# Six of the eight u blocks by a one-level Strassen product beside the first group's scores

## The chip, the cores and the metric

The kernel runs on one core of a Trainium2 chip. The metric is the device time of one launch in microseconds (us), as the median of several runs. All arithmetic is in float32.

## The reference, cut to what matters

Two layers over a graph of N = 4096 nodes with D = 512 features. The first is an attention layer whose scores get the adjacency matrix added twice, the second a two-step graph convolution; each has a residual and a layer norm.

```python
def _L0_gnn_ref(x, spatial_encoding, edge_encoding, Wq, bq, Wk, bk, Wv, bv):
    q = x @ Wq.T + bq
    k = x @ Wk.T + bk
    v = x @ Wv.T + bv
    a = q @ k.T * scale + spatial_encoding + edge_encoding
    attn = jax.nn.softmax(a, axis=-1)
    return attn @ v
def _L1_gnn_ref(x, adj, W1, b1, W2, b2):
    h = jax.nn.relu(adj @ (x @ W1) + b1)
    out = adj @ (h @ W2) + b2
    return out
x = _layernorm(x + _L0_gnn_ref(x, adj, adj, ...), axis=-1)
x = _layernorm(x + _L1_gnn_ref(x, adj, ...), axis=-1)
```

## The kernel before

The two projections of the scores are folded into one matrix: with m made of Wq and Wk, the scores of a block are x times u, where u = m applied to x, scaled, plus a bias (`ub_t`). u has eight blocks (`u_products(b)`, b = 0 to 7), one for each group of 512 rows of the result. A block is made by 16 matmuls of 512 columns: four output quarters o, four contraction pieces c. ScalarE moves each quarter from PSUM to SBUF with its bias (L190), and four subtractions (`combine_u`, L204) make of its quadrants B11, B12, B21 and B22 the sums T1 to T4. Block 0 stays in SBUF. Blocks 1 to 7 go through the tile `uo` to memory (`u_d`, L196) and come back seven operands at a time when their group begins (`load_operand`, L214). `uo` comes from a pool with one buffer (L133).

The scores themselves are one-level Strassen products. For each group g and each block d of 512 rows of x there are seven products k in `ORDER` = 1, 2, 6, 7, 5, 4, 3, each with a left operand out of plain quadrants of x (A11, A12, A22) and their sums (S1 to S4), and a right operand of u (B11, B21, B22, T1 to T4). `qk` (L344) makes half a product with two matmuls of 256 columns; the products add up in two PSUM banks, X for k = 1, 6, 5, 3 and Y for 2, 7, 4, and VectorE adds the running state of the bank to the right quadrant of the scores after each product (`qk_read`, L360). X has one buffer, and so has Y. For group 0 the sums S1 to S4 of each block d are made by VectorE (`form_s`, L225) from the loaded piece of x transposed (`XTS`, two buffers) and stored; later groups load them (`load_s`).

The order of the work is written out by hand. The main loop (from L1086) counts units. A unit has seven steps, a step is one half of a score product; two units make a score block, 16 units a group. `at(unit, n, f)` hooks a function to a step, and `work[unit] = units, items` gives a list of TensorE pieces with their costs, to be spread over so many units from there on: after each step as many are issued as keep the pace. Each engine runs its own instructions in the order in which the loop wrote them, and waits on semaphores where it needs another's result; so do the DMA queues of SP and GpSimd (POOL).

In group 0 the pieces beside the scores are the u products: blocks 1 to 5 in units 0 to 10, blocks 6 and 7 in units 11 to 17 (L816, L817). Unit 18 has none. After the last scores of group 0 (unit 15) its maxima are finished, transposed and spread (`turn_max` at unit 16, `spread_max` at unit 17), and for each pair q of score rows VectorE subtracts the maximum (`shift`), ScalarE takes the exponential (`exps`), GpSimd adds up the rows (`sums`) and makes the sums of a further Strassen product (`px_t2`), at places that the list `PREP` sets. From unit 19 on the products of the exponentials with x (`px_items`, L476, tile "p") fill the gaps, 224 pieces in 14 units; the tiles of x for them are loaded by `load_x` three phases ahead, into two pools of together four buffers (`xnp` with three, `xnp2` with one). In group 0, GpSimd and VectorE also make the row sums of x that these products need (`sum_x`, `row_parts`). At unit 18 the pools of the u stage are closed (`form.close()`), and the pools of the later stages take over their memory.

Of the kernel before, what the change touches and what calls it, by code (L numbers as in the profile page):

```python
# [11 lines left out]
F32 = mybir.dt.float32  # L12
AF = mybir.ActivationFunctionType
ALU = mybir.AluOpType
# [4 lines left out]
P = 128  # L19
# [5 lines left out]
def tile_graph_attention_then_gcn(  # L25
# [51 lines left out]
    nc = tc.nc  # L77
# [4 lines left out]
    NG = N // W  # L82
    NP = NT // 2
    HW = W // 2
    NCK = N // CW
    PER = W // P
    HALF_SCALE = 0.5 / math.sqrt(D)
# [14 lines left out]
    t_sb = const.tile([P, NT, H], F32, name="t_sb")  # L102
    c_sb = const.tile([P, NT], F32, name="c_sb")
    c0_t = const.tile([P, 1], F32, name="c0_t")
    ub_t = const.tile([P, ND], F32, name="ub_t")

    u_d = [dram.tile([P, 7, 2, HW], F32, name=f"u_d{g}") for g in range(NG)]
# [13 lines left out]
    att = ctx.enter_context(ExitStack())  # L121
# [2 lines left out]
    bcp = att.enter_context(tc.tile_pool(name="bcp", bufs=1, side="right"))  # L124
    small = att.enter_context(tc.tile_pool(name="small", bufs=4, side="right"))

    xnp = att.enter_context(tc.tile_pool(name="xnp", bufs=3, side="right"))
    form = ExitStack()
    mp = form.enter_context(tc.tile_pool(name="mp", bufs=1, side="right"))
    m_t = mp.tile([P, ND, D], F32, name="m_t")  # L130
    g_t = mp.tile([P, D], F32, name="g_t")
    xtp = form.enter_context(tc.tile_pool(name="xtp", bufs=2, side="right"))
    uop = form.enter_context(tc.tile_pool(name="uop", bufs=1, side="right"))  # L133

    def bank(tag, name, bufs=1):
        return psum.tile([P, W], F32, tag=tag, name=name, bufs=bufs)
# [10 lines left out]
    B11, B21, B22, T1, T2, T3, T4 = range(7)  # L147
    B12 = T4
    OPERANDS = {1: (A11, B11), 2: (A12, B21), 3: (S4, B22), 4: (A22, T4), 5: (S1, T1),
                6: (S2, T2), 7: (S3, T3)}  # L150
    ORDER = (1, 2, 6, 7, 5, 4, 3)

    FAST_V = range(NG - 2)
    QUARTER = {1: (0, 0), 2: (0, 0), 6: (1, 0), 7: (1, 1), 5: (1, 1), 4: (1, 0), 3: (0, 1)}
    L = {}
    UT, UO, XTS, SA, S, XN, CB, MB, MACC, LACC, O, OT, RL, XR, T = ({} for _ in range(15))


    def load_xts(b):
        XTS[b] = xtp.tile([P, ND, W], F32, tag="xt", name=f"xt{b}")  # L160
        nc.sync.dma_start(XTS[b], xT[:, ts(b, W)].rearrange("(c p) i -> p c i", p=P))

    def u_products(b):

        ps = {}

        def one(o, c):
            def go():
                if c == 0:
                    ps[o] = bank("o", f"psu{b}_{o}", 4)  # L170
                nc.tensor.matmul(  # L171
                    ps[o], m_t[:, c, ts(o, P)], XTS[b][:, c, :], start=c == 0, stop=c == ND - 1
                )
                if c == ND - 1:
                    if o == 0:
                        if b:
                            UO[b] = uop.tile([P, 7, 2, HW], F32, tag="ut", name=f"uo{b}")
                        else:
                            for k in ORDER:
                                new_operand(0, k)  # L180
                    pair = (B11, B12) if o < 2 else (B21, B22)
                    if b:
                        to = UO[b][:, pair[0] : pair[1] + 1 : pair[1] - pair[0], o % 2, :]
                        todo = [(to, ps[o].rearrange("p (h i) -> p h i", h=2))]
                    else:
                        todo = [
                            (UT[0, pair[h]][:, o % 2, :], ps[o][:, ts(h, HW)]) for h in range(2)
                        ]
                    for to, src in todo:
                        nc.scalar.activation(  # L190
                            to, src, AF.Identity, bias=ub_t[:, o : o + 1], scale=HALF_SCALE
                        )
                    if o == ND - 1:
                        if b:
                            combine_u(nc.gpsimd, {k: UO[b][:, k] for k in range(7)})
                            nc.gpsimd.dma_start(u_d[b], UO[b])  # L196
                        else:
                            combine_u(nc.vector, {k: UT[0, k] for k in range(7)})

            return go  # L200

        return [one(o, c) for o in range(ND) for c in range(ND)]

    def combine_u(eng, ut):  # L204
        for out_, a, b_ in ((T1, B12, B11), (T2, B22, T1), (T3, B22, B12), (T4, B21, T2)):
            eng.tensor_tensor(ut[out_], ut[a], ut[b_], ALU.subtract)
# [204 lines left out]

    def load_x(n):
        g, a, b, k = PHASES[n]
        pool = xnp2 if n % 4 == 3 else xnp
        XN[n] = pool.tile([P, b - a, 2 * P], F32, tag="xn", name=f"xn{n}")
        plain = {1: (0, 0), 2: (1, 0), 4: (1, 1)}
        if k in plain:
            t, f = plain[k]
            src = x.rearrange("(d t j p) f -> t p d j f", p=P, t=2, j=2)[t]
            for d in range(a // 2, b // 2):  # L420
                nc.sync.dma_start(
                    XN[n][:, 2 * d - a : 2 * d - a + 2], src[:, d, :, ts(f, 2 * P)]
                )
        else:
            nc.sync.dma_start(XN[n], xs_d[a][:, {6: 0, 7: 1, 3: 2, 5: 3}[k]])
# [282 lines left out]
    with tc.tile_pool(name="wqk", bufs=1) as wp:  # L708
# [52 lines left out]
        for w_t, w_n in ((wq_t, wq_n), (wk_t, wk_n)):  # L761
            for o in range(ND):
                ps = bank("o", f"psw{o}", 4)
# [43 lines left out]
    def at(unit, n, f, *args):  # L807
        n += unit * len(ORDER)
        hooks[n // len(ORDER), n % len(ORDER)].append(lambda: f(*args))
# [3 lines left out]
            f()  # L813

    work = {}
    work[0] = 11, [(0.86, f) for g in range(1, 6) for f in u_products(g)]  # L816
    work[11] = 7, [(0.86, f) for g in range(6, NG) for f in u_products(g)]  # L817
    for g in range(2, NG):
        at(max((g - 1) * ND * ND // 7 - 1, 0), 0, load_xts, g)

# [144 lines left out]
    def strassen(n, beside, done=()):  # L965
# [54 lines left out]
        (6, MID), (7, MID), (8, EARLY), (8, LATE), (9, MID), (10, MID), (11, MID), (12, MID),  # L1020
    ]

    PREP_LAST = [
        (1, (2, 2, 3)), (1, (3, 4, 4)), (1, (5, 6, 6)), (2, EARLY), (2, LATE), (3, LATE), (4, MID),
        *PREP[7:],
# [8 lines left out]
    for g in range(NG):  # L1034
        s0 = g * NP
        s1 = s0 + NP
        if g:
            for n, k in enumerate(ORDER):
                at(s0 - 2 + (2 * n + 1) // 7, (2 * n + 1) % 7, load_operand, g, k)
            at(s0 - 2 - (g == 1), 1, add_c0, g)  # L1040
            at(s0 - 2 - (g == 1), 3, row_consts, g)
        for q in range(NP):
            d, j = divmod(q, 2)
            if (g or d) and j == 0:
                early = 2 + (g == 1 and d == 0)
                at(s0 + q - early, 4, begin_scores, g, d)
                at(s0 + q - early, 5, add_scores, g, d)
            for h in range(2):
                n = 1 + 3 * (2 * j + h) if d < NP // 2 - 1 else 2 * j + h
                at(s0 + 2 * d + 2 + n // 7, n % 7, new_max, g, q, h)  # L1050
            unit, (n0, n1, n2) = (PREP_LAST if g == NG - 1 else PREP)[q]
            at(s1 + unit, n0, shift, g, q, 0)
            at(s1 + unit, n1, shift, g, q, 1)
            at(s1 + unit, n1, exps, g, q)
            at(s1 + unit, n2, sums, g, q)
            at(s1 + unit, n2, px_t2, g, q)
        at(s1, 5, turn_max, g)
        at(s1 + 1, 1, spread_max, g)
        if g < NG - 1:
            at(s1 + 13, 4, row_sums, g)  # L1060
        at(s1 + 14, 0, load_rows, g)
        at(s1 + 15, 0, add_bv, g)
        px = px_items(g)
        if g == NG - 1:
            for n, (u, k) in enumerate(spare):
                px.insert((8, 14, 20, 26, 90, 150)[n], (0.86, lambda u=u, k=k: product(u, k)))
        if g:
            px.reverse()
            by = 3 if g == NG - 1 else 1
            items = row_items(g - 1, lambda n: [px.pop() for _ in range(n * by)])  # L1070
            work[s1 + 1] = NP, items + px[::-1]
        else:
            work[s1 + 3] = NP - 2, px

    for n in range(3):
        at(NP + 1, 2 + n, load_x, n)

    last_unit = (NG + 1) * NP + 1
    at(last_unit - 5, 0, lambda: [sum_t(0, 0, 8), sum_t(8, 8, 14)])
# [6 lines left out]
    for unit in range(last_unit):  # L1086
        if unit == NP + 2:
            form.close()
            wvp = att.enter_context(tc.tile_pool(name="wvp", bufs=1, side="right"))
            bv_t = wvp.tile([P, D], F32, name="bv_t")  # L1090
            b2_t = wvp.tile([P, D], F32, name="b2_t")
            wv_t = wvp.tile([P, ND, D], F32, name="wv_t")
            w1_t = wvp.tile([P, ND, H], F32, name="w1_t")
            wvs_t = wvp.tile([P, 3, 2, HW], F32, name="wvs_t")
            v = wv_t.rearrange("p (f c) (h o) -> p f h c o", f=2, h=2)
            WV = {B11: v[:, 0, 0], T3: v[:, 0, 1], B21: v[:, 1, 0], B22: v[:, 1, 1]}
            WV.update({b: wvs_t[:, n] for n, b in enumerate((T1, T2, T4))})
            rowp = att.enter_context(tc.tile_pool(name="rows", bufs=1, side="right"))
            xnp2 = att.enter_context(tc.tile_pool(name="xnp2", bufs=1, side="right"))
        if unit == NP + 6:  # L1100
            nc.sync.dma_start(wv_t, wvT.rearrange("(c p) o -> p c o", p=P))
            nc.sync.dma_start(w1_t, w1.rearrange("(c p) h -> p c h", p=P))
# [36 lines left out]
    g = NG - 1  # L1139
# [171 lines left out]
```

## Time and profile before

| | us |
|---|---|
| median of 3 runs | 2329.12 |
| lowest and highest | 2328.04, 2330.17 |
| the profiled execution, its time | 2332.29 |
| its span, first to last instruction | 2330.5 |
| TensorE busy | 2298.2 |
| mean granted TensorE clock | 0.998 |

The page gives busy times of five engines: PE is TensorE's matmuls, PEld its weight loads, which overlap them, DVE VectorE, ACT ScalarE, POOL GpSimd; SP only issues transfers. A line of a group of instructions reads: line of the code, engine, operation, tile written and tiles read, shapes, count, then busy time and the mean in ns of one, then the idle time of the engine just before them and what ended it. In an order in time each line begins with the start and the duration in us, neighbours of one kind merged, and ends with the idle time before it in brackets, with its releaser. Numbers of buffers are left out of the names: `X` and `Y` are the score banks, `psu` the banks of the u products, `uo` the u tile on its way to memory, `p` the banks of the px products, `s` the score tiles.

### The profile page before, as it was taken

What the parts mean: (1) busy time and instruction counts of PE and PEld (TensorE: products, weight loads), DVE (VectorE), ACT (ScalarE), POOL (GpSimd) and SP (SyncE); (2) the same over time, 40 slices, a digit from 0 to 9 for tenths busy, and PEclk for the clock granted to TensorE, in tenths of its full rate; (3) what the DMA queues carried; (4) which work ended last, traced back from release to release, by engine and by line L of the source; (5) the groups of instructions that cost most, each with busy time, mean ns of one, the idle gap of its engine ahead of it and who ended that gap; (6) DMA issues with size and microseconds to landing.
All of it is one profiled execution on the core that took longest, in us unless ns stands there. A gap on an engine that the chain in (4) does not pass through costs nothing.

```text
span 2330.5 us, 28148 instructions
## 1 busy us (share of the span) xinstructions
PE 2298.2 (99%) x10518; PEld 1725.5 (74%) x10518; DVE 1615.2 (69%) x2270; ACT 399.1 (17%) x417; POOL 1004.8 (43%) x999
## 2 busy tenths in 40 slices
PE   9999999999999999999999999999999999999998
PEld 5666788888888888888888888888886743333456
DVE  4556665677678766865776676667757877888874
ACT  2111211131122112211311131121102100000012
POOL 1567654165328423741662185237419830011043
PEclk9999999999999999999999999999999999999999
DMA  5889787757757784778577667757654558899996
GB/s 155 261 279 306 230 228 192 220 146 218 216 154 210 199 233 131 216 193 232 129 233 200 180 188 202 226 144 216 185 184 157 179 218 311 330 354 371 344 387 224
DMA packets 276886, 523.27 MB, mean 225 GB/s; under 512 B 19152, under 2 KB 126416, under 8 KB 275856
## 3 DMA queue, kind: packets, MB, share of 16 engines
q1 hardware_dynamic: 229040, 406.12, 51.8%
q0 software_dynamic: 42176, 105.39, 20.5%
q10 hardware_dynamic: 5536, 9.97, 1.2%
q8 instruction: 84, 1.38, 0.2%
q14 instruction: 50, 0.41, 0.1%
HBM read 473.44 MB, written 46.40 MB: 223 GB/s over the span
## 4 chain that ended last, share of the span: by engine, by line
PE 91%; DVE 4%; POOL 2%; issue 1%; DMA 1%; ACT 0%; POOLq 0%; SPq 0%; DVEq 0%; ACTq 0%
PE p L491 31%; PE X L351 18%; PE b L957 14%; PE Y L351 13%; PE psu L171 4%; PE v L618 3%; PE acce L1256 2%; PE ops L1210 1%; PE tps L664 1%; PE x L566 1%; DVE s L441 1%; PE x1ps L655 1%; DVE s L364 1%; PE psm L774 1%; DVE s L446 1%
## 5 line engine op out<-in xcount | busy, mean ns | idle before, releaser
L491 PE MATMUL p<-s,xn 128*128 128x256 f32 x3584 | 895.5, 380 | 8.9 <-DVE s L441 5.9
L491 PEld LDWEIGHTS p<-s,xn 128*128 128x128 f32 x3584 | 677.7, 190 | 113.3 <-DVE s L441 9.1
L351 PE MATMUL X<-ut,sa 128*128 128x256 f32 x1984 | 513.8, 382 | 3.2 <-DVE s L364 3.2
L351 PEld LDWEIGHTS X<-ut,sa 128*128 128x128 f32 x1984 | 371.0, 190 | 87.8 <-issue 25.1
L407 POOL TENSOR_TENSOR lacc<-lacc,s 128x512 f32<-128x512 f32 x240 | 345.6, 1440 | 199.8 <-ACT s L398 188.9
L364 DVE TENSOR_TENSOR s<-X,s 128x512 f32<-128x512 f32 x256 | 176.2, 688 | 292.4 <-PE X L351 288.4
L351 PE MATMUL Y<-ut,sa 128*128 128x256 f32 x1408 | 360.9, 379 | 2.2 <-DVE s L364 1.8
L351 PEld LDWEIGHTS Y<-ut,sa 128*128 128x128 f32 x1408 | 266.3, 190 | 49.2 <-issue 12.2
L398 ACT ACTIVATE s<-s 128x1024 f32<-128x1024 f32 x128 | 135.2, 1057 | 803.4 <-DVE s L394 803.4
L373 DVE TENSOR_TENSOR macc<-macc,s 128x512 f32<-128x512 f32 x240 | 254.2, 1059 | 1.2
L364 DVE TENSOR_TENSOR s<-Y,s 128x512 f32<-128x512 f32 x192 | 132.0, 688 | 174.9 <-PE Y L351 174.1
L295 POOL DMA_DIRECT2D s<-in_adjT_dram x64 | 84.5, 1320 | 362.9 <-ACT s L290 359.1
L394 DVE TENSOR_TENSOR s<-s,mb 128x512 f32<-128x512 f32 x256 | 232.1, 916 | 2.5 <-ACT mb L321 2.5
L464 DVE TENSOR_TENSOR ot<-p,ot 128x512 f32<-128x512 f32 x248 | 169.0, 681 | 30.4 <-PE p L491 30.0
L924 DVE TENSOR_TENSOR tt<-ck 128x1024 f32<-128x1024 f32 x112 | 138.5, 1270 | 40.6 <-PE b L957 36.5
L957 PE MATMUL b<-tt,st 128*64 128x512 f32 (+1 forms) x768 | 156.1, 541 | 0.0
L171 PE MATMUL psu<-xt,m_t 128*128 128x512 f32 x256 | 128.0, 592 | 0.0
L441 DVE TENSOR_TENSOR s<-s 128x512 f32<-128x512 f32 x128 | 126.4, 1010 | 0.0
L434 POOL TENSOR_TENSOR s<-s 128x256 f32<-128x256 f32 x128 | 123.0, 961 | 0.6
L290 ACT COPY s<-cb 128x2048 f32<-128x2048 f32 x64 | 120.9, 1888 | 0.5
L957 PEld LDWEIGHTS b<-tt,st 128*64 128x64 f32 x768 | 53.9, 137 | 87.8 <-issue 79.4
L435 POOL TENSOR_TENSOR s<-s 128x256 f32<-128x256 f32 x128 | 107.1, 837 | 10.0
(165 smaller groups left out, 1971.6 us busy)
## 6 DMA issues: line engine op xcount, KB each, us to landing
ck<-in_adjT_dram SPq DMA_DIRECT2D x128, 1024.0 KB, 7.4
s<-in_adjT_dram POOLq DMA_DIRECT2D x64, 1024.0 KB, 11.6
sa<-s_d SPq DMA_DIRECT2D x224, 256.0 KB, 5.4
xn<-in_x_dram SPq DMA_DIRECT2D x192, 256.0 KB, 3.8
xn<-xs_d SPq DMA_DIRECT2D x96, 512.0 KB, 4.7
sa<-in_xT_dram SPq DMA_DIRECT2D x168, 256.0 KB, 4.7
xn<-xs_d SPq DMA_DIRECT2D x64, 256.0 KB, 4.0
u_d<-uo POOLq DMA_DIRECT2D x7, 1792.0 KB, 7.3
```

Of the source, the lines that this page charges most:

```text
L171: nc.tensor.matmul(ps[o], m_t[:, c, ts(o, P)], XTS[b][:, c, :], start=c == 0, stop=c == ND - 1)
L351: nc.tensor.matmul(T["X" if k in (1, 6, 5, 3) else "Y"][:, ts(j, HW)], SA[g, d, a][:, c, j, :], UT[g, b][:, c, :], start=k in (1, 2, 7) an ...
L364: nc.vector.tensor_tensor(ck, ps, ck, ALU.add)
L373: nc.vector.tensor_tensor(MACC[g], MACC[g], ck[:, h, :], ALU.max)
L394: nc.vector.tensor_tensor(ck, ck, MB[g], ALU.subtract)
L398: nc.scalar.activation(ck, ck, AF.Exp, scale=2.0)
L407: nc.gpsimd.tensor_tensor(LACC[g], LACC[g], ck[:, h, :], ALU.add)
L441: nc.vector.tensor_tensor(b, b, t2, ALU.subtract)
L464: nc.vector.tensor_tensor(to, ps, to, ALU.add)
L491: nc.tensor.matmul(T["PX" if k in (1, 6, 5, 3) else "PY"][:, ts(f, HW)], XN[n][:, q - a, ts(f, P)], quarters(g, q)[{1: 0, 2: 2, 6: 1, 7: 0 ...
L924: nc.vector.tensor_tensor(t[:, :2], v[:, :, 1], v[:, 0], ALU.subtract)
L957: nc.tensor.matmul(BK[n][k][ts(half, HH)], lhs, right(u, i, half, b), start=q == 0, stop=q == NP - 1,)
```

## The change

Blocks 2 to 7 of u are no longer made by `u_products` but by `u_fast`: seven products of quadrants of x with quadrants of m, with the same left sums S1 to S4 that the scores of group 0 use for the same block of x, and with sums of m as right operands. Each half of a product is two matmuls of 256 columns. Two banks add up as in `qk`, and after each product its state is read into or added to a quadrant: by ScalarE where it is the first to write there (k = 1, 6, 7, 3), by VectorE where it adds (k = 2, 5, 4). The last read of a block is put off to the first piece of the next (`owing`). GpSimd makes T1 to T3 as before, VectorE T4. The u tile is split: B11 has a tile of its own with two buffers, the other six operands share one with one buffer, and `store_u` sends both.

`m_sums` makes T1, T2 and T4 of m on GpSimd at unit 1, `m_t3` makes T3 in place on VectorE at unit 3. Block 1 is made as before, in units 0 to 2; blocks 2 to 7 in units 3 to 15. The px products of group 0 begin a unit sooner and take 15 units, the first two pairs of `PREP` are moved to unit 17 for group 0, block 1 of group 1's scores is begun a unit sooner, and of the four buffers for tiles of x two are now in each pool.

```diff
-    xnp = att.enter_context(tc.tile_pool(name="xnp", bufs=3, side="right"))
+    xnp = att.enter_context(tc.tile_pool(name="xnp", bufs=2, side="right"))
...
+    ms_t = mp.tile([P, 2, 2, HW], F32, name="ms_t")
...
+    def new_uo(b, what):
+
+        if what == B11:
+            UO[b] = {B11: uop.tile([P, 2, HW], F32, tag="b11", name=f"b11_{b}", bufs=2)}
+        else:
+            UO[b]["all"] = uop.tile([P, 6, 2, HW], F32, tag="ut", name=f"uo{b}")
+            UO[b].update({k: UO[b]["all"][:, k - 1] for k in range(1, 7)})
+
+    def store_u(b):
+        nc.gpsimd.dma_start(u_d[b][:, B11], UO[b][B11])
+        nc.gpsimd.dma_start(u_d[b][:, 1:], UO[b]["all"])
+
+    def m_sums():
+
+        m = m_t.rearrange("p (f c) (h o) -> p f h c o", f=2, h=2)
+        for k, v in ((B11, m[:, 0, 0]), (T3, m[:, 0, 1]), (B21, m[:, 1, 0]), (B22, m[:, 1, 1])):
+            MV[k] = v
+        MV[T1] = t_sb[:, 28:32, :].rearrange("p (c a) b -> p c (a b)", c=2)
+        MV[T2], MV[T4] = (ms_t[:, n] for n in range(2))
+        for out_, a, b_ in ((T1, T3, B11), (T2, B22, T1), (T4, B21, T2)):
+            nc.gpsimd.tensor_tensor(MV[out_], MV[a], MV[b_], ALU.subtract)
+
+    def m_t3():
+
+        nc.vector.tensor_tensor(MV[T3], MV[B22], MV[T3], ALU.subtract)
+
+    def u_fast(b):
+
+
+        X = {}
+
+        def read(k):
+            ps = X["X" if k in (1, 6, 5, 3) else "Y"].rearrange("p (o i) -> p o i", o=2)
+            if k == 1:
+                new_uo(b, B11)
+            if k == 6:
+                new_uo(b, "all")
+            to = UO[b][{1: B11, 2: B11, 6: B12, 4: B12, 7: B22, 5: B22, 3: B21}[k]]
+            if k in (1, 6, 7, 3):
+                for n in range(2):
+                    o = n + 2 * (k in (7, 3))
+                    nc.scalar.activation(
+                        to[:, n, :], ps[:, n], AF.Identity, bias=ub_t[:, o : o + 1], scale=HALF_SCALE
+                    )
+            else:
+                nc.vector.scalar_tensor_tensor(to, ps, HALF_SCALE, to, ALU.mult, ALU.add)
+            u = UO[b]
+            if k == 4:
+                for out_, a, b_ in ((T1, B12, B11), (T2, B22, T1), (T3, B22, B12)):
+                    nc.gpsimd.tensor_tensor(u[out_], u[a], u[b_], ALU.subtract)
+            if k == 3:
+                nc.vector.tensor_tensor(u[T4], u[B21], u[T2], ALU.subtract)
+                store_u(b)
+
+        def one(k, j):
+            def go():
+                if j == 0 and k in (1, 2, 7):
+                    X["X" if k == 1 else "Y"] = bank("o", f"psu{b}_{k}", 4)
+                for c in range(2):
+                    nc.tensor.matmul(
+                        X["X" if k in (1, 6, 5, 3) else "Y"][:, ts(j, HW)],
+                        MV[OPERANDS[k][1]][:, c, ts(j, P)],
+                        SA[0, b, OPERANDS[k][0]][:, c],
+                        start=k in (1, 2, 7) and j == 0 and c == 0,
+                        stop=c == 1,
+                        skip_group_check=True,
+                    )
+                if j == 0:
+                    if k == 1:
+                        if owing:
+                            owing.pop()()
+                    else:
+                        read(ORDER[ORDER.index(k) - 1])
+                elif k == 3:
+                    owing.append(lambda: read(3))
+
+            return go
+
+        return [one(k, j) for k in ORDER for j in range(2)]
...
-        pool = xnp2 if n % 4 == 3 else xnp
+        pool = xnp2 if n % 4 > 1 else xnp
...
-    work[0] = 11, [(0.86, f) for g in range(1, 6) for f in u_products(g)]
-    work[11] = 7, [(0.86, f) for g in range(6, NG) for f in u_products(g)]
+    work[0] = 3, [(0.86, f) for f in u_products(1)]
+    work[3] = 13, [(0.86, f) for g in range(2, NG) for f in u_fast(g)] + [(0, lambda: owing.pop()())]
+    at(1, 0, m_sums)
+    at(3, 0, m_t3)
...
+    PREP_FIRST = [(1, (2, 3, 4)), (1, (4, 5, 6)), *PREP[2:]]
...
-                early = 2 + (g == 1 and d == 0)
+                early = 2 + (g == 1 and d < 2)
...
-            unit, (n0, n1, n2) = (PREP_LAST if g == NG - 1 else PREP)[q]
+            unit, (n0, n1, n2) = {0: PREP_FIRST, NG - 1: PREP_LAST}.get(g, PREP)[q]
...
-            work[s1 + 3] = NP - 2, px
+            work[s1 + 2] = NP - 1, px
...
-        at(NP + 1, 2 + n, load_x, n)
+        at(NP + n // 2 + 1, 2 + n if n < 2 else 0, load_x, n)
...
-            xnp2 = att.enter_context(tc.tile_pool(name="xnp2", bufs=1, side="right"))
+            xnp2 = att.enter_context(tc.tile_pool(name="xnp2", bufs=2, side="right"))
```

More of the change, by code (lines that the diff above doesn't have):

```diff
@@ L155, in tile_graph_attention_then_gcn @@
     L = {}
+    MV, owing = {}, []
     UT, UO, XTS, SA, S, XN, CB, MB, MACC, LACC, O, OT, RL, XR, T = ({} for _ in range(15))
@@ L176, in go @@
                         if b:
-                            UO[b] = uop.tile([P, 7, 2, HW], F32, tag="ut", name=f"uo{b}")
+                            new_uo(b, B11)
+                            new_uo(b, "all")
                         else:
@@ L181, in go @@
                     pair = (B11, B12) if o < 2 else (B21, B22)
[L182 to L189, printed above, removed]
-                        nc.scalar.activation(
-                            to, src, AF.Identity, bias=ub_t[:, o : o + 1], scale=HALF_SCALE
+                    for h in range(2):
+                        nc.scalar.activation(
+                            (UO[b][pair[h]] if b else UT[0, pair[h]])[:, o % 2, :],
+                            ps[o][:, ts(h, HW)],
+                            AF.Identity,
+                            bias=ub_t[:, o : o + 1],
+                            scale=HALF_SCALE,
                         )
@@ L194, in go @@
                         if b:
-                            combine_u(nc.gpsimd, {k: UO[b][:, k] for k in range(7)})
-                            nc.gpsimd.dma_start(u_d[b], UO[b])
+                            combine_u(nc.gpsimd, UO[b])
+                            store_u(b)
                         else:
```

## The prediction

> **What bounds the kernel now.** First the page, for the engine that sets the end.
>
> ```profile
> PE 2298.2 (99%) x10518; PEld 1725.5 (74%) x10518; DVE 1615.2 (69%) x2270; ACT 399.1 (17%) x417; POOL 1004.8 (43%) x999
> ...
> PE 91%; DVE 4%; POOL 2%; issue 1%; DMA 1%; ACT 0%; POOLq 0%; SPq 0%; DVEq 0%; ACTq 0%
> ...
> L171 PE MATMUL psu<-xt,m_t 128*128 128x512 f32 x256 | 128.0, 592 | 0.0
> ```
>
> TensorE is idle for 32 us of 2330.5 and carries 91% of the chain that ended last: taking products away shortens the run unless waits fill the place. Matmul durations on the page are latencies of a pipelined unit; what one costs is the spacing of starts, so next the order in time on TensorE (start us, us, ... xcount, idle before):
>
> ```profile
> 32.45 10.46 PE L171 MATMUL psu<-xt,m_t 128*128 128x512 f32 x24
> 42.75 1.03 PE L351 MATMUL X<-ut,xt 128*128 128x256 f32 x4
> ```
>
> 24 records in 10.30 us are 0.429 us each. A float32 matmul makes two records (L171 counts 256 for the 8 x 16 matmuls of the code), so one of 512 columns costs 0.858 us. Now the same view where the u products end and the attention-times-x products ("p") begin:
>
> ```profile
> 251.91 1.03 PE L351 MATMUL X<-ut,sa 128*128 128x256 f32 x4
> 253.72 1.99 PE L351 MATMUL X<-ut,sa 128*128 128x256 f32 x8 [0.78 <-DVE s L364]
> 255.55 1.89 PE L351 MATMUL Y<-ut,sa 128*128 128x256 f32 x8
> 257.28 1.89 PE L351 MATMUL X<-ut,sa 128*128 128x256 f32 x8
> 260.96 1.99 PE L351 MATMUL Y<-ut,sa 128*128 128x256 f32 x8 [1.79 <-DVE s L364]
> 262.79 1.03 PE L491 MATMUL p<-s,xn 128*128 128x256 f32 x4
> ```
>
> From 255.55 to 257.28 eight records take 1.73 us: a matmul of 256 columns costs 0.4325 us. And unit 18 (from 253.72), the one unit with nothing beside the scores, shows what such a unit suffers: VectorE can't read the score banks in time, 0.78 and 1.79 us. The busy time by stretch, columns as in the page (us, then PE, PEld, DVE, ACT, POOL busy, clock, DMA share, GB/s):
>
> ```profile
> 150.00:200.00 50.00, 49.29 (x176) 33.05 (x176) 32.30 (x53) 7.93 (x9) 31.47 (x31) 1.00 0.87 267
> ...
> 254.00:276.00 22.00, 18.88 (x86) 15.95 (x86) 19.22 (x19) 6.02 (x6) 21.05 (x18) 1.00 0.75 223
> ```
>
> While u is made, TensorE is full and VectorE 65% busy; around unit 18 VectorE is 87% busy and TensorE loses 3 us of 22. Last, the tile that u passes through on its way to memory:
>
> ```profile
>   DMA u_d<-uo: 50.0, 4
> ...
> DMA to landing us min/median/max: 6.5/7.3/10.1
> ```
>
> ScalarE waited 50 us in four pieces for the store of the previous block to free the one buffer. No stall of TensorE goes with them: between 42 and 232 us it shows one, 0.71 us.
>
> **What the Trainium skill says.** "TensorE: Matmul & The Clock Gate", section "What's actually happening": after an idle window of about 3.4 us the array's clock is halved until it has been busy for as long. The trace has such a piece: after a 1.92 us wait at 301.34 ten records take 3.46 us (302.26 to 305.72) instead of 10 x 0.216 = 2.16, so a drop cost 1.3 us; the idle time before it was shorter than a window. "SBUF — State Buffer", section "Who interferes with whom": a VectorE instruction with two SBUF inputs and a GpSimd instruction that reads SBUF shut each other out. The trace agrees: the running maxima (L373) take 0.68 us alone and 1.06 on average.
>
> **The change, part by part.**
>
> (a) TensorE work. Per block, 16 matmuls of 512 columns (16 x 0.858 = 13.73 us) become 7 products x 2 halves x 2 = 28 of 256 (28 x 0.4325 = 12.11). The saving is 1.62 us, for six blocks 9.7 us. All of it lies where TensorE is full, so it counts whole: -9.7.
>
> (b) Reads of the u banks. ScalarE: 8 activations of 256 columns (0.47 us each, the row of ut) = 3.8 us a block in place of 4 x 0.69 = 2.7; it is below 20% busy here, nothing. VectorE gains three reads of PSUM plus SBUF (0.69, as L364) and one subtraction of two SBUF tiles (1.06, as L373): 3.1 us per block of 14 x 1.80 = 25.2 us, so its share goes from 65% to 77%. GpSimd loses one of four subtractions (1.6) and gains three once (4.8 us, in the second unit). Their cover is TensorE's other items: a product is read while the scores and the next product run, and its bank is written again at the earliest two items, 3.6 us, later. The tight place is the border of two score blocks, where the one X bank is read by VectorE with one u item (0.87 us) between. The trace of before has one stall there in 16 units, 0.71 us. With 12 points more load I take one more, 0.7 us (bounds 0 and 4); the wait of VectorE for the last plain u matmul before it overwrites m: 0.4.
>
> (c) The wait of ScalarE for the store. The six derived tiles still have one buffer. From the end of block b's last product: GpSimd is through with T1 to T3 after 2.7 us, the B11 store's issue 0.6, the large store's landing 7.3, ScalarE's next read 0.9: 11.5 us. TensorE needs that read at the fifth product of block b+1, eight items on: 8 x 1.80 + 0.87 = 15.3 us. Slack 3.8. For block 6, four subtractions of the row sums stand before the store on GpSimd (3.5 us): slack 0.3, I take a stall of 0.3. From block 1, still made the old way: after ScalarE 0.9, three subtractions 4.6, issues 1.2, landing 7.3, read 0.9 and a few tenths of signals, 15.3, against 17 pieces x 0.866 = 14.7: 0.6. Behind the waiting read on ScalarE stand the copies that begin later scores, needed two units on. So (b) and (c): +2.0, bounds 0 and 6.
>
> (d) Units 16 to 18. Before, 32 u items fill units 11 to 17, unit 18 is bare. Now u ends with unit 15, units 16 and 17 are bare (0.866 us a step), and the p products start with unit 18. Walk VectorE's order from the end of the last u product (T = 0), TensorE otherwise continuous: last X read till -0.1; a maximum till 1.0; T4, which waits for GpSimd's subtractions (second done at 1.1, third at 2.7), till 1.9 or 3.5; a maximum till 2.8 or 4.4; first read of the new X till 3.5 or 5.1, wanted at 3.56; two maxima till 5.0 or 6.7; the transposes of the maximum, wanted at 4.5 or 6.0, wait 0.5 to 1.3. Together 1.3 (T4 waits for two) or 3.0 (for three). In unit 17 the subtraction of the row maximum needs its broadcast through TensorE and ScalarE; four of them (0.68 each, 0.97 on average in this stretch) and four reads then fill VectorE, so the last X read comes 0.9 to 2.0 late. Sum 2.2 to 5.0, I take 3.6. In its place go 0.39 (a load, in unit 16) + 0.78 + 1.79 = 2.96. Net +0.6, bounds -0.8 and +2.
>
> (e) What moves without a price. The loads of x tiles keep four buffers in all (3 + 1 becomes 2 + 2); the third is loaded at unit 18 from a pool that waits for block 7's store, about 14 us after T = 0 and before unit 18 ends up needing it; behind it on SP stand loads wanted a unit later. The score loads of block 1 of group 1 start a unit sooner. The p products of group 0 are spread over 15 units instead of 14, the same number; the waits at 273.78, 277.47 and 301.34 (1.33, 0.83, 1.92) come from the hand-over from GpSimd to VectorE in two-row phases and stay. SP's loads of score operands for units 16 and 17 have less time per product (1.73 us against 7.0 to 7.5 to land), but stand seven products ahead, 12 us.
>
> Sum: -9.7 + 2.0 + 0.6 = -7.1 us. The span 2330.5 becomes 2323.4; with the 1.8 us outside the span (2332.3) the profiled run is 2325.2; the median lies 3.2 below its profiled run, so 2322.0.
>
> **The rivals.** *The bare units cost more.* For: three waits there pass from engine to engine, and idle pieces in sequence can bring the clock down. Against: unit 18 of before had 2.6 us of stalls at full clock. Price: 5.0 + two drops of 1.3 in place of 2.96, i.e. +4.6, and +2: -3.1, time 2326.0.
>
> *The store decides (slower).* If the one buffer comes free too late, TensorE stops in each of the six hand-overs. It needs the large store to land 7.3 + 3.8 = 11.1 us after its issue before TensorE loses anything; to end over 0.2% slower (+4.7) it has to lose 14.4 us, 2.4 per hand-over, a landing of 13.5 us, or 12.2 if each stall also brings a clock drop. For it: DMA is 87% busy here, and the 1 MB accumulating loads take 11.6. Against: seven stores took 6.5 to 10.1. Time at 13.5: 2334.
>
> *Everything fits.* No stall while u is made, unit 16 to 18 at the lower bound, and 1.5 us of the waits after 270 gone because the p products start more slowly: -9.7 - 0.8 - 1.5 = -12, 2317.1.
>
> **How the numbers follow.** Forecast 0.58, bare units 0.22, store 0.10, all fits 0.10. A measurement of this kernel tells 0.2%, 4.7 us, from no change. Forecast and "all fits" are faster: 0.68; bare units fall within: 0.22; the store is slower: 0.10. The range takes in the first, second and nearly the last: 2317.0 to 2330.0, the upper end being all upper bounds of (b) to (d) with some clock drops (-9.7 + 6 + 2 + 2.6 = +0.9).
>
> **What would show it.** The matmul group of u: 6 x 56 = 336 records of 256 columns, 64 of 512. Unit 18 starts some 7 us before 253.72. No wait of TensorE on ScalarE's or VectorE's u reads over 1 us; stalls of 2 to 5 us between the last u product and the first p product, named after VectorE. The time from the first p product to the end equal to before's within 2 us. I am wrong if TensorE waits in most hand-overs of u blocks, if the clock in that stretch falls below 0.97, or if the stretch after 330 us changes.

## The result, and the profile after

| | before | changed |
|---|---|---|
| median, us | 2329.70 (22 runs) | 2326.43 (22 runs) |
| lowest and highest | 2327.59, 2333.14 | 2323.25, 2328.72 |
| profiled execution: time, span | 2332.29, 2330.5 | 2326.35, 2324.6 |

The ratio of the changed kernel to the one before is 0.9984, with a 95% interval of 0.9977 to 0.999: 3.3 us less between the medians, where 7.1 were forecast. It lies in the range, but under the 0.2% that the forecast's own case called for. The first pair of profiles shows 5.9 us; the kernel before had been profiled in an execution 2.6 us above its median.

The page of the changed kernel, busy times and the chain:

```profile
PE 2288.3 (98%) x10662; PEld 1752.4 (75%) x10662; DVE 1631.5 (70%) x2295; ACT 403.7 (17%) x445; POOL 1006.0 (43%) x1003
...
PE 90%; DVE 4%; POOL 3%; issue 1%; DMA 1%; ACT 0%; POOLq 0%; SPq 0%; DVEq 0%; ACTq 0%
```

TensorE's busy time fell by 9.9 us, about what the products should give (9.7), the span by 5.9. So 4 us came back as idle time. Below is TensorE's order in time in the changed kernel: its longer waits from the u stage (the stretch in which u is made) up to the start of the p products.

```profile
183.90 1.28 PE L431 MATMUL X<-ut,xt 128*128 128x256 f32 x4 [2.09 <-DVE s L444]
184.97 1.91 PE L224 MATMUL psu<-xt,m_t 128*128 128x256 f32 x4
186.68 1.76 PE L431 MATMUL X<-ut,xt 128*128 128x256 f32 x4
188.28 1.03 PE L224 MATMUL psu<-xt,m_t 128*128 128x256 f32 x4
...
211.04 1.13 PE L431 MATMUL X<-ut,xt 128*128 128x256 f32 x4 [1.03 <-DVE s L444]
...
227.13 1.13 PE L224 MATMUL psu<-sa,t_sb 128*128 128x256 f32 x4 [2.87 <-ACT uo L206]
...
242.77 1.13 PE L431 MATMUL X<-ut,sa 128*128 128x256 f32 x4 [1.37 <-DVE s L444]
244.51 0.66 PE L458 MATMUL mt<-ident,macc 128*128 128x128 f32 x4 [0.60 <-DVE macc L453]
...
254.58 1.13 PE L431 MATMUL X<-ut,sa 128*128 128x256 f32 x4 [0.78 <-DVE s L444]
255.54 1.03 PE L571 MATMUL p<-s,xn 128*128 128x256 f32 x4
```

Unit 18 begins at 254.58, not 7 us before the 253.72 of the kernel before, but 0.9 us after it: all of the saving was gone by then. Yet p begins with it, in a unit that had been bare, and from there the changed kernel gains.

Two kinds of hand-over took the saving: from 40 to 239 us TensorE waits 4.1 us for VectorE to read the X bank, and 3.4 us for ScalarE to read a u bank. After the first long wait the clock dropped as well: the twelve records from 183.90 to 188.28 take 4.38 us, where twelve take 12 x 0.2165 = 2.60 elsewhere in this stretch (four in 0.866). That is another 1.8 us.

The ScalarE waits come from the tile of u on its way to memory:

```profile
  DMA u_d<-uo: 36.1, 4
...
DMA to landing us min/median/max: 5.8/10.2/10.9
```

The stores land after 10.2 us in the median (7.3 before). GpSimd's order between blocks 6 and 7 shows the hand-over with the longest wait, and the fence after it ScalarE's read that waited:

```profile
206.90 2.95 POOL L214 TENSOR_TENSOR uo<-uo 128x512 f32<-128x512 f32 x2
209.78 1.32 POOL L375 DMA_DIRECT2D s<-in_adjT_dram  x1
210.63 1.23 POOL L354 TENSOR_TENSOR t_sb<-t_sb 128x256 f32<-128x256 f32 x1
...
215.47 0.55 POOL L175 DMA_DIRECT2D u_d<-uo  x1
```

```profile
226.24 1.57 ACT L206 ACTIVATE uo<-psu,ub_t 128x256 f32<-128x256 f32 x4 [12.32 <-DMA u_d<-uo]
```

The subtractions for T1 to T3 end at 209.85, but the large store is issued only at 215.47, behind the issue of a 1 MB load and four subtractions of the row sums. It lands 10.7 us later, ScalarE goes on at 226.24, and TensorE stops for 2.87 us. The landing is not what sets this hand-over apart: the large stores of blocks 3 to 5 landed after 10.6, 10.9 and 10.2 us, with waits of at most 0.55 us on TensorE. But block 5's, for one, was issued 1.0 us after its last subtraction (181.30 to 182.32), block 6's 5.6 us after. Why the landings grew from 7.3 us is not shown.

The other place is the border of two score blocks, where the X bank passes from one to the next. VectorE's order at the one of 183.90:

```profile
178.43 1.74 DVE L453 TENSOR_TENSOR macc<-macc,s 128x512 f32<-128x512 f32 x1
180.09 0.68 DVE L444 TENSOR_TENSOR s<-Y,s 128x512 f32<-128x512 f32 x1
181.33 0.69 DVE L216 TENSOR_TENSOR uo<-uo 128x512 f32<-128x512 f32 x1 [0.56 <-POOL uo L214]
181.94 0.68 DVE L410 SCALAR_TENSOR_TENSOR t_sb<-t_sb,g_t 128x512 f32<-128x512 f32 x1
...
182.55 0.69 DVE L319 TENSOR_TENSOR sa<-xt,sa 128x512 f32<-128x512 f32 x1
183.16 0.68 DVE L444 TENSOR_TENSOR s<-X,s 128x512 f32<-128x512 f32 x1
```

Ahead of the last read of the X bank (183.16) stand a maximum that takes 1.74 us while GpSimd's subtractions run (178.03 to 181.30; the next maximum, at 183.88, takes 0.69), T4 with a wait of its own (L216), a row sum and S4 (L319). TensorE, which needs X for the next block, had been waiting since 181.8.

### The profile page after: what moved, and what is told of

It reads as the page before. It is cut to its first block, busy times and chain, and to the rows that moved or that the text cites. A ratio compares the mean times of both kernels' runs of the same rounds, so it can differ in the third digit from the quotient of the medians.

```text
span 2324.6 us, 28492 instructions
## 1 busy us (share of the span) xinstructions
PE 2288.3 (98%) x10662; PEld 1752.4 (75%) x10662; DVE 1631.5 (70%) x2295; ACT 403.7 (17%) x445; POOL 1006.0 (43%) x1003
## 4 chain that ended last, share of the span: by engine, by line
PE 90%; DVE 4%; POOL 3%; issue 1%; DMA 1%; ACT 0%; POOLq 0%; SPq 0%; DVEq 0%; ACTq 0%
PE p L571 31%; PE X L431 17%; PE b L1039 15%; PE Y L431 13%; PE v L698 3%; PE acce L1339 2%; PE psu L224 1%; PE ops L1293 1%; PE tps L744 1%; PE psu L253 1%; PE x L646 1%; POOL uo L214 1%; PE x1ps L735 1%; DVE s L521 1%; DVE s L444 1%
## 5 line engine op out<-in xcount | busy, mean ns | idle before, releaser
L484 POOL TENSOR_TENSOR lacc<-s 128x512 f32<-128x512 f32 x8 | 10.6, 1322 | 201.7 <-ACT s L478 201.7
## 6 DMA issues: line engine op xcount, KB each, us to landing
s<-in_adjT_dram POOLq DMA_DIRECT2D x64, 1024.0 KB, 11.1
```

## The experiments

In the runs below each time stands beside that of the kernel before from the same session, which lay between 2328.80 and 2329.47 us. Across sessions the differences to it are compared, not the times.

**Is it one execution's luck?** Both kernels were profiled again.

> The changed kernel once more, for a second profile. In the first one TensorE lost 7.5 us to waits while u was made (4.1 at the borders of score blocks behind VectorE, 3.4 behind ScalarE's wait for the store) and 1.4 us in all from the first p product to 330 us, where the kernel before had lost 4.1 and a clock drop. Theory A (hand-overs eat the saving, the earlier start of the p products gives it back): the waits of the u stage are again 6 to 10 us, those after the first p product again under 2 us. Theory B (one execution's luck): either sum comes out changed by half or more. Time by both: 3 to 4 us below before.

Measured 2325.97 us (before 2329.47; ratio 0.9984, 0.9977 to 0.999). Who waited for whom on TensorE from 40 to 239 us (in total, times, longest), and TensorE's order after the longest wait:

```profile
PE X L431 <- DVE s L444: 3.9, 3, 2.1
PE psu L224 <- ACT uo L206: 3.1, 1, 3.1
```

```profile
223.99 1.38 PE L224 MATMUL psu<-sa,t_sb 128*128 128x256 f32 x4 [3.13 <-ACT uo L206]
225.16 1.91 PE L431 MATMUL X<-ut,sa 128*128 128x256 f32 x4
226.87 1.67 PE L224 MATMUL psu<-sa,t_sb 128*128 128x256 f32 x4
228.37 1.03 PE L431 MATMUL X<-ut,sa 128*128 128x256 f32 x4
```

Again 7.0 us of waits in the two places. After the wait of 3.13 twelve records take 4.38 us (223.99 to 228.37) instead of 2.60: a clock drop again cost 1.8 us, but in another place. In this execution there was none after the 2.10 us wait at 182.19, the twin of the one that brought it in the first profile.

> The kernel before once more, for a second profile of the stretch from 246 to 330 us. If its waits there are a property of the kernel: again 5 to 8 us in all (0.8 and 1.8 around unit 18, three of 0.8 to 1.9 in the first px phases), a clock drop or not. If the first profile was an unlucky one: under 3 us.

A single execution, 2328.47 us. TensorE's order:

```profile
251.74 2.00 PE L351 MATMUL X<-ut,sa 128*128 128x256 f32 x8 [0.78 <-DVE s L364]
...
258.97 2.00 PE L351 MATMUL Y<-ut,sa 128*128 128x256 f32 x8 [1.79 <-DVE s L364]
...
271.79 1.13 PE L491 MATMUL p<-s,xn 128*128 128x256 f32 x4 [1.32 <-DVE s L441]
275.47 1.13 PE L351 MATMUL X<-ut,sa 128*128 128x256 f32 x4 [0.83 <-DVE s L364]
...
299.35 0.70 PE L491 MATMUL p<-s,xn 128*128 128x256 f32 x2 [1.92 <-DVE s L441]
```

The kernel before has the same five waits to within 0.01 us (6.6 us together), and no clock drop this time. These waits belong to the program, the drops to the execution. Two more waits behind VectorE repeat as exactly: 0.98 us (at 334.68 in the first profile) and 0.64 (387.57).

Now these two executions, spans 2326.7 and 2323.2, stage by stage, before and changed. From the first score product to unit 18 they take 210.64 and 211.33 us: 0.69 more, where the products save 9.7. From unit 18 to the first product with Wv in group 1 they take 200.15 and 193.63: 6.52 less. From there to the last product the changed kernel takes 0.58 more, its last transfer ends 1.06 later after that, and its first score product began 0.69 later. The sum is -3.50.

**The two halves of the change, one by one.** First the new u without the earlier start of p:

> The Strassen u as changed, but the px products start at unit 19 over 14 units, the first two pairs are prepared at units 17 and 18 and block 1 of group 1 is begun as before, so that units 16 to 18 have nothing beside the scores. Theory A: the Strassen u by itself is worth little (-9.7 of matmuls, +7.5 of waits, +1.5 in the bare units), the px hand-over costs what it cost before: before +0 to +3 us, the changed kernel +4 to +6 us. Theory B: the early start of px is worth nothing: as the changed kernel within 1.5 us.

```diff
-    PREP_FIRST = [(1, (2, 3, 4)), (1, (4, 5, 6)), *PREP[2:]]
+    PREP_FIRST = PREP
-                early = 2 + (g == 1 and d < 2)
+                early = 2 + (g == 1 and d == 0)
-            work[s1 + 2] = NP - 1, px
+            work[s1 + 3] = NP - 2, px
```

(The new split of the x buffers stays.) 2336.01 us (before 2329.47; ratio 1.0024, 1.0017 to 1.0032): slower than both, and more than expected. TensorE's order, then the busy times of the stretch (us, PE, PEld, DVE, ACT, POOL, clock, DMA share, GB/s):

```profile
262.01 3.78 PE L431 MATMUL X<-ut,sa 128*128 128x256 f32 x8 [4.35 <-DVE s L444]
```

```profile
256.00:276.00 20.00, 15.65 (x61) 13.07 (x60) 9.07 (x14) 5.45 (x5) 12.58 (x12) 0.83 0.76 198
```

With three bare units in a row the wait in unit 18 becomes 4.35 us, and the clock drops (0.83 in this stretch). By itself the new u, with its bare units, is a loss of 6.5 us: without the earlier start of p the change would have been slower than the kernel before. Then the moves without the new u:

> The u products as before (sixteen of 512 columns a block), spread evenly over units 0 to 15, with the moves of the change alone: px from unit 18 over 15 units, first pairs prepared at unit 17, pools of x tiles two and two. Theory A: 4 to 7 us below before, as fast as the changed kernel or faster, since it gains at the hand-over to px and has no waits in the u stage. Theory B: as before within 1.5 us.

```diff
-    work[0] = 11, [(0.86, f) for g in range(1, 6) for f in u_products(g)]
-    work[11] = 7, [(0.86, f) for g in range(6, NG) for f in u_products(g)]
+    work[0] = 16, [(0.86, f) for g in range(1, NG) for f in u_products(g)]
...
-            work[s1 + 3] = NP - 2, px
+            work[s1 + 2] = NP - 1, px
```

(and the preparation, the early block and the two pools as in the change). 2323.23 us, ratio 0.9973 (0.9962 to 0.9983): 6.2 us below before, and 2.7 below the changed kernel of the same session (2325.97). So the whole gain of the change is that of its moves; the Strassen product itself had bought nothing so far. From the first score product to unit 18 this kernel, with the old products, takes 211.33 us, as long as the changed kernel did in its second profile: what the new products save there went into waits and a clock drop. Where the 2.7 us lie is not shown: the two profiles differ by 1.8, all of it outside this stretch. TensorE has no wait from 42 to 240 us; all of them from 239 to 460:

```profile
PE mt L378 <- DVE macc L373: 1.5, 1, 1.5
PE X L351 <- DVE s L364: 0.8, 1, 0.8
PE p L491 <- DVE ot L464: 0.6, 1, 0.6
PE p L491 <- DVE s L441: 0.5, 2, 0.3
PE p L491 <- DMA xn<-in_x_dram: 0.2, 1, 0.2
```

**What of the moves it is.**

> The kernel before with the earlier preparation alone: the first two pairs in unit 17 and block 1 of group 1 begun a unit sooner; px still from unit 19, unit 18 bare. If VectorE's load in unit 18 is what cost: the waits around unit 18 (2.6 us) go, the later ones stay, 2 to 3 us below before. If it is the start of px in unit 18 that counts: as before within 1 us.

2328.50 us, ratio 0.9996 (0.9987 to 1.0004). TensorE's order:

```profile
272.62 1.50 PE L491 MATMUL p<-s,xn 128*128 128x256 f32 x4 [3.36 <-DMA xn<-xs_d]
...
300.74 0.70 PE L491 MATMUL p<-s,xn 128*128 128x256 f32 x2 [1.92 <-DVE s L441]
```

The wait of 1.79 us in unit 18 is gone, but TensorE waits 3.36 us for a tile of x before the fourth p phase, and the later waits, 1.92, 0.98 and 0.64, are there as before. The time is the one expected if the start of p counts, but part of it comes from that new wait, which neither expectation had.

> The kernel before with the moves of the px start alone, its u products left where they were (units 0 to 10 and 11 to 17), so that no unit is without pieces beside the scores; the run with u spread over units 0 to 15 and two bare units was 6.2 us below before. If bare units are what costs: the 2.3 us of waits in units 16 and 17 go too, 7 to 9 us below before. If the p tiles' load, whose memory block 7's u tile holds until its store has landed, comes too late instead: a wait for that load of 3 us or more, no gain over the other run.

2333.21 us, ratio 1.0014 (1.0008 to 1.0021). TensorE's order, and SP's queue:

```profile
268.67 1.19 PE L491 MATMUL p<-s,xn 128*128 128x256 f32 x2 [7.65 <-DMA xn<-xs_d]
```

```profile
247.07 0.37 SPq L252 DMA_DIRECT2D sa<-in_xT_dram  x1
264.61 0.81 SPq L425 DMA_DIRECT2D xn<-xs_d  x2
```

SP stands still for 17 us: the load of the third x tile goes to memory that block 7's u tile holds until its store, issued at 258.51, has landed. Behind it the other loads wait too. The second expectation came true: started in unit 18 while u ends in unit 17, p has to wait for this load. After that stop the waits are 0.28, 0.27 and 0.56 us, as in the changed kernel. A stop of 7.65 us could have cleared them by itself, so this run alone proves little. But over all runs it holds without exception: with p from unit 18 (old or new u) the later waits are these three, with p from unit 19 (old u, new u, or the preparation alone) the waits of 1.92, 0.98 and 0.64 are there.

**The wait for the store.**

> The changed kernel with B12 in a tile of its own with two buffers and B11 with one, its store sent as soon as B11 is ready, so that ScalarE's first write of a block into the shared tile comes two pieces later. Theory A: the waits of TensorE on ScalarE's u reads (3.4 us) go, 2 to 4 us below the changed kernel; the waits behind VectorE at the block borders stay at 3 to 5 us. Rival (the landing of the store is bound by the transfers as a whole, so that the wait only moves to the next read): within 1 us of the changed kernel, the wait on ScalarE turning up at the seventh product.

```diff
+        elif what == B12:
+            UO[b][B12] = uop.tile([P, 2, HW], F32, tag="b12", name=f"b12_{b}", bufs=2)
...
-        nc.gpsimd.dma_start(u_d[b][:, B11], UO[b][B11])
-        nc.gpsimd.dma_start(u_d[b][:, 1:], UO[b]["all"])
+        nc.gpsimd.dma_start(u_d[b][:, 1:6], UO[b]["all"])
+        nc.gpsimd.dma_start(u_d[b][:, B12], UO[b][B12])
...
             if k == 6:
+                new_uo(b, B12)
+                nc.gpsimd.dma_start(u_d[b][:, B11], UO[b][B11])
+            if k == 7:
                 new_uo(b, "all")
```

(B11 with one buffer, the shared tile with five operands: the same memory. The large store is a sixth smaller too.) 2320.14 us, ratio 0.9957 (0.9945 to 0.997), 5.8 below the changed kernel of the same session. TensorE's waits from 40 to 239 us:

```profile
PE X L438 <- DVE s L451: 5.3, 4, 2.1
PE mt L465 <- DVE macc L460: 0.6, 1, 0.6
```

The waits on ScalarE are gone, those behind VectorE are where they were (the 5.3 us now include the 1.4 of unit 16, which comes before 239 us). From the first score product to unit 18 this kernel takes 208.30 us instead of 211.33: 3.0 less, the length of the wait. Why the medians differ by 5.8 is not shown.

**VectorE's queue at the borders.** Two moves, each alone on the changed kernel and then on top of the version with B12 in two buffers. S4 behind the read of X, and T4 back to GpSimd:

```diff
-                at(2 * d - 2, 4 + 3 * n, lambda d, n: formed[d][n](), d, n)
+                at(2 * d - 2, 4 + 3 * n + n // 3, lambda d, n: formed[d][n](), d, n)
```

```diff
-                nc.vector.tensor_tensor(u[T4], u[B21], u[T2], ALU.subtract)
+                nc.gpsimd.tensor_tensor(u[T4], u[B21], u[T2], ALU.subtract)
```

> The changed kernel with one move: VectorE forms S4 of a score block one step later, behind the last read of the X bank instead of ahead of it. Theory A1 (the border waits are VectorE's queue: what stands ahead of that read): the waits of 2.10 and 1.03 us at the borders of blocks lose 0.7 us or more each, so 1.5 to 2.5 us of TensorE's waits behind VectorE go, 1 to 3 us below the changed kernel. A2 (the borders wait for a late product or for a piece missing beside the scores): the waits stay, within 0.5 us of the changed kernel.

2326.32 us, ratio 0.9987 (0.9981 to 0.9994), 2.5 below before where the changed kernel was 3.3 and 3.5 below: no gain. TensorE's order:

```profile
182.04 1.13 PE L431 MATMUL X<-ut,xt 128*128 128x256 f32 x4 [1.50 <-DVE s L444]
...
224.51 2.08 PE L224 MATMUL psu<-sa,t_sb 128*128 128x256 f32 x4 [4.34 <-ACT uo L206]
```

The border waits fell from 3.9 to 2.3 us, about as A1 had it (2.10 to 1.50, 1.02 to nothing), but the waits on the store rose from 3.1 to 5.7: a TensorE that comes sooner waits longer for the same store. The clock drop after the wait of 4.34 is longer as well: twelve records take 5.28 us (224.51 to 229.79). Neither expectation had this.

> The changed kernel with T4 of u made by GpSimd again. VectorE no longer stands still for GpSimd's subtractions in its queue, but the store goes out 1.3 us later. A1: the waits of 2.10 and 1.38 us (where VectorE waits 0.6 and 1.2 us for T4's operands) lose 1 us or more each, while the wait of ScalarE's u read on the store (3.1 us) grows by about 1: in sum within 1.5 us of the changed kernel. If T4 plays no part: waits behind VectorE as they were, 1 us slower by the store.

2325.94 us, ratio 0.9987 (0.9981 to 0.9994), 2.9 below before. The wait of 1.38 in unit 16 is gone, the one at 183.78 is 2.39 us, no better, and the waits on the store are 4.2 (3.1). In sum nothing, as expected, but only one of the two waits answered.

> B12 in two buffers (as in the run with the tile of its own) and S4 one step later. If the two waits are independent and add up: the 9.3 us below before of the first and the 1 to 3 us of the second, 10 to 12 us below before. If they replace each other: as with B12 alone, within 0.7 us.

2317.02 us, ratio 0.9946 (0.9934 to 0.9959), 11.8 below before: the two add up once the store is out of the way.

> As the last, and T4 on GpSimd: with the buffer of B12 doubled the later store costs nothing, so what is left of the waits behind VectorE while u is made is under 1.5 us and the time is 0.5 to 2 us below the version without this; 11 to 13 us below before. If T4 plays no part: within 0.5 us of it.

2315.37 us, ratio 0.9938 (0.9925 to 0.995): the best version, 13.4 us below before. TensorE's waits from 40 to 239 us:

```profile
PE X L438 <- DVE s L451: 1.5, 2, 0.8
PE psu L229 <- ACT uo L211: 0.7, 1, 0.7
PE mt L465 <- DVE macc L460: 0.4, 1, 0.4
PE Y L438 <- DVE s L451: 0.4, 1, 0.4
PE psu L229 <- DVE uo L215: 0.2, 1, 0.2
```

The waits behind VectorE while u is made are about 2 us, where under 1.5 was expected; the border wait of 2.10 has come down to 1.50 by the move of S4 and to 0.71 by that of T4. The moves alone were 6.2 us below before, this version is 13.4 below, 7.2 more: most of the 9.7 us of the new products arrives. The traces agree: from the first score product to unit 18 it takes 204.47 us, 6.9 less than the moves alone.

## Why the prediction was right or wrong, point by point

The range and the direction held; the size did not, and the direction held by luck. The terms of the sum against what the two pairs of profiles show, in us:

| term | forecast | measured |
|---|---|---|
| (a) fewer products | -9.7 | -9.7 |
| (b), (c) waits while u is made | +2.0 | +6.8 |
| clock drop there | not counted | +1.8 |
| (d) units 16 to 18 | +0.6 | -0.2 |
| (e) waits after the start of p | 0 | -4.6 |
| sum | -7.1 | -5.9 |

The medians differ by 3.3. The second pair of profiles, which differs by 3.5, has the missing 2.4 us outside these terms: in the start, after group 0 and in the last transfer. What causes them is open.

- **The step that failed is the price of the hand-overs, (b) and (c): +2.0, bounds 0 and 6.** They cost 6.8 us more than in the kernel before, in both pairs, and brought a clock drop of 1.8 us that the prediction had put into a rival alone. With them the u stage gained nothing.
- (a), the saving of 9.7 us: right. The u group has 336 records of 256 columns and 64 of 512, and TensorE's busy time fell by 9.9.
- (b), VectorE at the borders: the place and the mechanism were right, the size wrong, 4.1 and 3.9 us where the kernel before had 0.7 and 0.2, and one more wait of 0.7 (at most 4) was forecast. The step counted VectorE's load (77%) and took one more stall like the one of before. It did not look at the order ahead of the border's read, where S4 and T4 stand: moving these two took the longest wait from 2.10 to 0.71. The wait for m, put at 0.4, doesn't appear.
- (c), ScalarE's wait for the store: again the right place, block 6, where the slack was put at 0.3 and a stall at 0.3. The wait was 2.87 and 3.13. Two parts of the sum were short: the landing, taken at 7.3 from the kernel before, was 10.7; and the large store went out 5.6 us after the last subtraction of u, where 4.1 stood (3.5 + 0.6), since the four subtractions took 4.3 and the issue of the 1 MB load ahead of them was left out. Of the wait behind block 1 (0.6) there is no sign.
- (d), the bare units: 2.75 us (1.37, 0.60, 0.78) against 3.6 taken, 2.2 to 5.0 as bounds. In its parts the walk holds only roughly: VectorE did wait for the third subtraction (1.16 us), a case for which unit 16 was put at 3.0, and lost 1.97 there; unit 17 was put at 0.9 to 2.0, and lost 0.78.
- (e), "the same number" of p products, the waits "stay": wrong, to the good. It counted the work that moves and not what it moves away from. With p in unit 18 the waits of 1.3, 0.8, 1.9, 0.98 and 0.64 become 0.28, 0.27 and 0.56. This is the luck: without these 4.6 us, which had been put at nothing, the measured -3.3 would be +1.3 (an estimate from the two figures), and without the moves altogether the new u was 6.5 us slower than the kernel before.
- The rivals: the bare units alone did not cost more. The store did decide in part, but in one hand-over and not in six. Of "everything fits" only the waits after 270 came true, and by 4.6 us rather than 1.5.
- Of the signs, three spoke against the forecast: unit 18 began 0.9 us later and not 7 earlier (the forecast's own terms give nearer 5: -9.7 + 2.0 + 3.6 - 0.39 - 0.78 = -5.3), a wait on ScalarE's u read was over 1 us, and the stretch after 330 us changed (the waits of 0.98 and 0.64 are gone). Two did not: TensorE waited in one or two hand-overs of u blocks and not in most, and the granted clock from 40 to 240 us was 0.99.

That it is the start of p in unit 18 that spares the later waits is shown as far as single parts go: the earlier preparation without it leaves them, and so does the new split of the x buffers without it (the first of the two halves above kept that split). The preparation and the split together, without the start, were not run. How the start does it is not settled; which of VectorE's pieces no longer meet was not followed.

## What to carry to other kernels

When the engine that bounds a kernel loses work, look at each buffer that another engine hands back to it, and at the order of that engine's queue ahead of the hand-over. The kernel before hid these with slack (ScalarE waited 50 us for the store, and TensorE didn't notice); with an eighth less of u products, made on another schedule, two kinds of them cost the saving. Of two such waits in a row, mending the first may show nothing, because the second grows (S4 alone), while mending the second shows at once (B12) and lets the first count. And price a moved stage by the stalls at the place it leaves and the place it goes to, not by its work alone, which is the same in both.

## What the runs showed of the hardware that was not expected

Behind VectorE, around and after unit 18, the waits of one program repeat from execution to execution to about 0.01 us (0.78, 1.79, 1.92). Others move: the wait on the store was 2.87 and 3.13 us, a border wait of the kernel before 0.71 and 0.23.

A clock drop is a matter of the execution. After 1.92 us of idle time ten records took 3.46 us in the first profile of the kernel before, and none were slow in the second; the changed kernel dropped after a wait of 2.09 us in one profile and not after 2.10 in the other. Such a drop cost 1.3 to 1.8 us in the profiles of these two kernels, and 2.7 after the wait of 4.34 us with S4 moved.

The same store of u landed after 5.7 to 11.1 us in the two profiles of the changed kernel. No run here tells why.
